# A conditioned transformer block: a quarter of fw1 reloaded, block 1's second LayerNorm a stage sooner, weight sums spread over three stages

## The chip, the core and the metric

The kernel runs on one core of one Trainium2 chip. The core has five engines that run at the same time, each with its own queue of instructions, which it takes strictly in order: TensorE (PE, matrix products; its weight loads are shown apart as PEld), VectorE (DVE), ScalarE (ACT), GpSimd (POOL) and SyncE (SP, which here only starts DMAs). An instruction whose inputs aren't there yet holds up everything behind it on its engine. The metric is the device time of one execution in microseconds (us), the median of three runs. In the profile, L599 means line 599 of the kernel's file.

## The reference

All data are float32. `x` is (2, 2048, 512), `t` (2, 512), and `h` = 1024. Cut to what is computed:

```python
emb = silu(t) @ ada_w + ada_b
shift_msa, scale_msa, gate_msa, shift_mlp, scale_mlp, gate_mlp = split(emb, 6)
norm = ln(x) * (1 + scale_msa) + shift_msa
x = x + gate_msa * (gelu(norm @ ssm_w1 + ssm_b1) @ ssm_w2 + ssm_b2)
norm2 = ln(x) * (1 + scale_mlp) + shift_mlp
x = x + gate_mlp * (gelu_tanh(norm2 @ ff_w1 + ff_b1) @ ff_w2 + ff_b2)
```

`ln` subtracts the mean of a row and divides by its standard deviation. The matrices are `ssm_w1`, `ssm_w2` (512 x 512; `w1`, `w2` in the kernel), `ff_w1` (512 x 1024; `fw1`) and `ff_w2` (1024 x 512; `fw2`).

## The kernel before

**Blocks and stages.** The 4096 rows of x are eight blocks of 512 rows (numbered 0 to 7; 0 to 3 belong to the first of the two conditions). Each block goes through four matrix stages, named after their tiles: hA (first product with w1, and gelu), oA (product with w2, added to x), hC (product with fw1, and gelu) and oC (product with fw2, added to x). TensorE runs them as hA_0, oA_0, hA_1, oA_1, hC_0, hA_2, oC_0, hC_1, oA_2, oC_1, hA_3 and so on, so that the vector work of one block lies beside the products of another.

**Products of halves.** A stage doesn't multiply whole matrices. Both operands are cut into quarters, called "11", "12", "21" and "22", and seven products P1 to P7 of quarters and of sums of quarters replace eight. `group` (L371) issues them in the order P1, P2, P6, P5, P7, P3, P4. P1, P6, P7 and P4 add into one bank of PSUM (y), P5 and P3 into another (v), P2 has its own (x). After each product `after` reads the bank: this is called a *take* here. Because the next product of the same bank adds into it, TensorE may start P6 only when P1's take has read, P7 only after P6's, P3 after P5's, and P4 after P7's. In hA and hC the takes are in `hidden` (L539), on VectorE, with gelus on ScalarE; in oA and oC they are in `residual` (L585), which adds into x on VectorE (L599).

**Sums.** Each operand needs four sums of quarters. `sums_of_first` (L307) writes "s1", then overwrites quarter "21" with "21" + "22", then writes "s0" and "s2"; `sums_of_second` (L316) writes "s1", overwrites "12", then writes "s0" and "s2". P6 reads "s0", P7 "s1", and P5 the overwritten quarter. For fw1 these four run once, on GpSimd, 128x1024 each (L310 to L313 with tiles `fw`, `fw_s`); likewise for fw2 (L320 to L323), after its eight k-slices were multiplied by the gate row (`fold5(0, 8)`, VectorE, L354; `fold5(8, 12)` are the four sums).

**Blocks 1 to 7 take another scheme for hC.** Instead of two groups of seven products, `Second.products` (L668) issues 26 smaller products (list `HK_P`), of 28 registers `fa` made from fw1 and 28 registers `fb[i]` made from the block's normalized rows. Registers 0 to 15 of `fa` are pieces of fw1 itself and 16 to 27 lie in the tile of its sums. Both are changed in place, by 37 sums of 128x256 for fw1 (`HK_A`, once, on VectorE, L634 and L636) and 20 sums for each block's rows (`HK_B`, on GpSimd for block 1). `HK_A` needs fw1 as it was loaded, not with its overwritten quarter, so fw1 is loaded a second time; and it can only begin when hC_0 no longer reads fw1.

**Second LayerNorm.** For block i, `Norm(i, 2)` (`n2[i]`) takes statistics of x (VectorE, four times L420 and L421), `scales` (eight tiny instructions on GpSimd, L429 to L447), four `normal` (ScalarE, L460), four `turn` (VectorE, 32x32 transposes into the tile `blocks`, L471), `move` (16 DMAs that finish the transposition, L480), and four `moved` (ScalarE, scale and shift, L503). The first LayerNorm of a block (`n1[i]`) goes the same way; for blocks 0 and 1 `normal(..., on_pe=True)` is followed by transposes on TensorE (`turned`).

**The order of the work around the products is written out by hand.** `hook(hooks, places, ops)` puts one operation after another behind the products named in `places` (the last place takes all that are left over). `group` calls them right after the product's take, and each lands in its engine's queue at that point. So a line such as `hook(hooks, ("P2", "P6", "P6", "P5"), st)` fixes where in VectorE's queue four statistics stand, and `take(n)` hands out the next n of the 37 sums of fw1.

Before the change the 37 sums stand as 4 in hA_2, 5 + 24 in oC_0 and 4 in hC_1.

## Time and profile before

| | us |
|---|---|
| median of three runs (615.16, 616.75, 614.74) | 615.16 |
| the profiled execution | 614.97 |
| its span, first to last instruction | 613.2 |

The profiled execution has some 1.8 us outside its span. The stages that the change touches, by the start of their first product: oA_0 at 30.19, hA_1 46.64, oA_1 59.92, hC_0 75.15 (its second half 87.75), hA_2 100.21, oC_0 112.30, hC_1 146.29, oA_2 170.34. Eight matmuls of 128x256 make one product of hA, oA or hC_0; undisturbed, products follow each other at 1.73 us (hA_2: 100.21, 101.94, 103.66, ...). In oC a product has sixteen matmuls and takes 3.45.

A timeline line reads: start, duration, engine, line, operation, tile written <- tiles read, shapes, count; in square brackets the idle time before it and who ended it. A line of a waits view reads: who <- on whom, us in total, how many times, the longest. A line of a windows view gives a stretch from:to, its length, the busy time of each engine in it with the count of instructions, TensorE's granted clock (1.00 is full), and DMA figures.

### The profile page before, as it was taken

What the parts mean: (1) busy time and instruction counts of PE and PEld (TensorE: products, weight loads), DVE (VectorE), ACT (ScalarE), POOL (GpSimd) and SP (SyncE); (2) the same over time, 40 slices, a digit from 0 to 9 for tenths busy, and PEclk for the clock granted to TensorE, in tenths of its full rate; (3) what the DMA queues carried; (4) which work ended last, traced back from release to release, by engine and by line L of the source; (5) the groups of instructions that cost most, each with busy time, mean ns of one, the idle gap of its engine ahead of it and who ended that gap; (6) DMA issues with size and microseconds to landing.
All of it is one profiled execution on the core that took longest, in us unless ns stands there. A gap on an engine that the chain in (4) does not pass through costs nothing.

```text
span 613.2 us, 8130 instructions
## 1 busy us (share of the span) xinstructions
PE 594.4 (97%) x2827; PEld 510.8 (83%) x2827; DVE 379.0 (62%) x641; ACT 216.6 (35%) x357; POOL 394.6 (64%) x445
## 2 busy tenths in 40 slices
PE   7999899968999999999999999999999999999997
PEld 4778788856888888888888888888888888888886
DVE  5968766999855456455666448744575336467642
ACT  3234335211641346222543236313462324212320
POOL 2866486996758399366996398895993695640110
PEclk9999999979999999999999999999999999999999
DMA  8980224221041201521022430413011310012001
GB/s 326 414 325 12 59 57 147 68 73 69 0 138 40 99 1 39 185 68 68 2 66 90 140 137 1 138 34 104 0 41 30 85 53 0 1 42 96 0 1 68
DMA packets 23371, 50.88 MB, mean 83 GB/s; under 512 B 4340, under 2 KB 4896, under 8 KB 22436
## 3 DMA queue, kind: packets, MB, share of 16 engines
q1 hardware_dynamic: 19648, 44.05, 21.3%
q10 hardware_dynamic: 3684, 6.33, 3.7%
q8 instruction: 22, 0.36, 0.2%
q14 instruction: 17, 0.14, 0.1%
HBM read 27.29 MB, written 8.39 MB: 58 GB/s over the span
## 4 chain that ended last, share of the span: by engine, by line
PE 84%; DVE 10%; issue 2%; DMA 2%; POOL 1%; ACT 1%; SPq 0%; POOLq 0%; DVEq 0%; ACTq 0%
PE py_oC L386 16%; PE px_hC L698 9%; PE pv_oC L386 8%; PE pv_hC L698 8%; PE py_hA L386 8%; PE py_hC L698 7%; PE py_oA L386 7%; PE pv_hA L386 4%; PE px_oC L386 4%; PE pv_oA L386 4%; DVE fw_s L636 2%; PE px_hA L386 2%; PE py_hC L386 2%; DVE fw L636 2%; PE px_oA L386 2%
## 5 line engine op out<-in xcount | busy, mean ns | idle before, releaser
L611 POOL TENSOR_TENSOR x<-x,gb 128x512 f32<-128x512 f32 x64 | 80.1, 1286 | 5.9 <-issue 2.1
L503 ACT ACTIVATE nT<-nT,mod,mod 128x512 f32<-128x512 f32 x54 | 39.6, 803 | 115.4 <-DMA nT<-blocks 115.4
L429 POOL TENSOR_SCALAR ve<-mv 128x4 f32<-128x4 f32 x16 | 3.7, 232 | 100.0 <-DVE mv L421 94.0
L386 PE MATMUL py_oC<-fw_s,hSC 128*128 128x256 f32 x256 | 59.6, 387 | 5.8 <-DVE x L599 5.8
L460 ACT ACTIVATE nT<-x,nmr,rstd 128x512 f32<-128x512 f32 x56 | 42.4, 803 | 55.7 <-POOL nmr L447 39.9
L386 PEld LDWEIGHTS py_oC<-fw_s,hSC 128*128 128x128 f32 x256 | 49.6, 195 | 13.5 <-DVE x L599 6.0
L310 POOL TENSOR_TENSOR hSC<-hClo 128x512 f32<-128x512 f32 x15 | 19.3, 1284 | 46.5 <-ACT hClo L693 37.8
L599 DVE TENSOR_TENSOR x<-py_oC,x 128x512 f32<-128x512 f32 (+1 forms) x36 | 22.5, 628 | 39.9 <-PE py_oC L386 39.9
L420 DVE BATCH_NORM_STATS2 st<-x 128x6 f32<-128x512 f32 x64 | 43.5, 679 | 5.0 <-DMA x<-in_x_dram 4.8
L698 PE MATMUL py_hC<-forms,fw 128*128 128x256 f32 x168 | 40.8, 379 | 0.0
L471 DVE STREAM_TRANSPOSE blocks<-nT 128x512 f32<-128x512 f32 x56 | 37.9, 694 | 3.9 <-ACT nT L460 3.4
L715 DVE TENSOR_TENSOR hClo<-hClo,py_hC 128x512 f32<-128x512 f32 x42 | 28.5, 681 | 17.0 <-ACT hClo L712 9.4
L636 POOL TENSOR_TENSOR forms<-forms 128x256 f32<-128x256 f32 x48 | 35.6, 741 | 2.8
L698 PEld LDWEIGHTS py_hC<-forms,fw 128*128 128x128 f32 x168 | 31.9, 190 | 4.3
L599 DVE TENSOR_TENSOR x<-py_oA,x 128x512 f32<-128x512 f32 x32 | 22.1, 690 | 20.5 <-PE py_oA L386 19.9
L715 DVE TENSOR_TENSOR hChi<-hChi,pv_hC 128x512 f32<-128x512 f32 x35 | 23.4, 684 | 17.1 <-PE pv_hC L698 17.1
L386 PE MATMUL py_oA<-w_s,hSA 128*128 128x256 f32 x128 | 30.4, 381 | 2.0 <-DVE hSA L312 2.0
L386 PE MATMUL py_oC<-fw_s,hChi 128*128 128x256 f32 x128 | 29.0, 380 | 1.7 <-DVE x L599 1.7
L386 PE MATMUL py_hA<-nS,w_s 128*128 128x256 f32 x128 | 30.3, 380 | 0.0
L386 PEld LDWEIGHTS py_oA<-w_s,hSA 128*128 128x128 f32 x128 | 24.2, 190 | 6.2 <-DVE hSA L312 2.4
L693 ACT ACTIVATE hClo<-hClo,colsT 128x256 f32<-128x256 f32 x56 | 25.3, 500 | 10.7 <-DVE hClo L715 10.5
L386 PE MATMUL pv_oC<-fw,hClo 128*128 128x256 f32 x128 | 28.9, 379 | 0.0
(228 smaller groups left out, 1429.0 us busy)
## 6 DMA issues: line engine op xcount, KB each, us to landing
nT<-blocks SPq DMA_DIRECT2D x160, 64.0 KB, 2.0
out_dram<-x SPq DMA_DIRECT2D x15, 512.0 KB, 3.0
x<-in_x_dram SPq DMA_DIRECT2D x7, 1024.0 KB, 7.1
ada<-in_L_cond_ada_w_dram SPq DMA_DIRECT2D x6, 1024.0 KB, 9.5
fw<-in_L_cond_ff_w_dram SPq DMA_DIRECT2D x3, 2048.0 KB, 9.0
nT<-blocks ACTq DMA_DIRECT2D x64, 64.0 KB, 2.1
w<-in_L_cond_ssm_w_dram SPq DMA_DIRECT2D x3, 1024.0 KB, 7.5
fw<-in_L_cond_ff_w_dram ACTq DMA_DIRECT2D x1, 2048.0 KB, 7.8
```

The source lines that it names most:

```text
L310: lambda: eng.tensor_tensor(s[1], q["11"], q["21"], ALU.subtract),
L386: nc.tensor.matmul(ps[b][j * apart][:, j, :], lhs(p, j, k), rhs(p, j, k), start=(fresh and j * (not apart) == 0 and k == 0), stop=(p in (" ...
L420: nc.vector.bn_stats(st, xs[self.i][:, c, :])
L460: nc.scalar.activation(t, x_c, AF.Identity, bias=self.nmr[:, c : c + 1], scale=self.rstd[:, c : c + 1])
L471: nc.vector.transpose(self.bl[:, :, :, c, :].rearrange("p m k q -> p k m q"), self.nT[:, c, :].rearrange("p (k m q) -> p k m q", k=KD, m=C),)
L503: nc.scalar.activation(dst, src, AF.Identity, bias=shift, scale=scale)
L599: nc.vector.tensor_tensor(d, ps[BANK[p]][:, js], d, ALU.add)
L611: lambda c=c: nc.gpsimd.tensor_tensor(xs[i][:, c, :], xs[i][:, c, :], gb, ALU.add)
L636: eng.tensor_tensor(reg[d], reg[a], reg[b], ALU.add if f == "+" else ALU.subtract)
L693: nc.scalar.activation(h, h, AF.Gelu_apprx_tanh, bias=fb1T[:, m : m + 1])
L698: nc.tensor.matmul(ps[b][:, j, :], fa[ra][:, j * P : (j + 1) * P], fb[rb].rearrange("p a (c q) -> p c a q", q=Q), start=(fresh and j == 0) ...
L715: nc.vector.tensor_tensor(dest(d), dest(d), ps[b], op)
```

## The change

It consists of these edits:

- **oA_0:** of n1[1]'s four `normal`, c = 0 and 2 stay on ScalarE behind P2; c = 1 and 3 go to VectorE (a `tensor_scalar`, L464), behind P6. fw1's third sum comes behind P4 of oA_0 (it stood in hA_1), its fourth behind P6 of oA_1.
- **oA_1:** on GpSimd, the first of n2[0]'s sums now stands ahead of n1[2]'s scales, the others behind; three of the eight folds of fw2 come here.
- **hC_0, first half:** block 1's statistics and scales, and the other five folds.
- **hC_0, second half:** block 1's four `normal` at once behind P1, its four `turn` and `move` (now all 16 DMAs on SP, before 8 on SP and 8 on ScalarE's queue); fw2's first sum ahead of n1[2]'s sums, the other three behind them; and `fw1_quarter`, which loads only quarter "21" of fw1 again (0.5 MB), where the whole 2 MB was loaded in hA_2.
- **hA_2:** block 1's `moved`; ten of the 37 sums on VectorE; the takes of P1, P6 and P5 go to ScalarE (`on_act`), two instructions each.
- **oC_0:** 18 of the sums; `HK_B` behind P1, the biases of block 2 behind P3. **hC_1:** the nine that are left.

```diff
+    def hidden(name, rhs, wops, bT, func, lo, hi, g, hooks, order=ORDER, on_act=False):
...
+        def take_first(dst, src, r):
+            if on_act:
+                for j in range(2):
+                    b = bT[:, r * half + m0 + j : r * half + m0 + j + 1]
+                    nc.scalar.activation(dst[:, j], src[:, j], AF.Identity, bias=b)
+            else:
+                nc.vector.tensor_tensor(dst, src, bias(r), ALU.add)
...
             if p == "P1":
-                nc.vector.tensor_tensor(s1, ps["y"], bias(0), ALU.add)
+                take_first(s1, ps["y"], 0)
...
             elif p == "P6":
-                nc.vector.tensor_tensor(u2, ps["y"], bias(0), ALU.add)
+                take_first(u2, ps["y"], 0)
             elif p == "P5":
-                nc.vector.tensor_tensor(s5, ps["v"], bias(1), ALU.add)
+                take_first(s5, ps["v"], 1)
...
-    hook(hooks, ("P2",), hA_sums[3:] + [lambda c=c: n1[1].normal(c, on_pe=True) for c in range(C)])
+    hook(hooks, ("P2",), hA_sums[3:] + [lambda c=c: n1[1].normal(c, on_pe=True) for c in (0, 2)])
+    hook(hooks, ("P6",), [lambda c=c: n1[1].normal(c, nc.vector) for c in (1, 3)])
     hook(hooks, ("P6",), [lambda: modulation(3, 1)])
...
     hook(hooks, ("P2",), fw1_sums[:1])
-    hook(hooks, ("P5",), fw1_sums[1:2])
+    hook(hooks, ("P5", "P4"), fw1_sums[1:3])
     residual("oA_0", 0, hA[0], w2_ops, KD // 2, hooks, order=FIRST)
...
-    hook(hooks, ("P2",), biases(1, gb[2]) + fw1_sums[2:])
+    hook(hooks, ("P2",), biases(1, gb[2]))
...
+    hook(hooks, ("P6",), fw1_sums[3:])
     hook(hooks, ("P2", "P6", "P6", "P5"), st)
-    hook(hooks, ("P5",), [n1[2].scales])
     hook(hooks, ("P6",), n2[0].moved())
-    hook(hooks, ("P5",), [ff_gate])
-    hook(hooks, ("P7",), n2[0].summed(nc.gpsimd) + [lambda c=c: n1[2].normal(c) for c in range(C)])
+    n2_sums = n2[0].summed(nc.gpsimd)
+    hook(hooks, ("P5",), [ff_gate] + n2_sums[:1] + [n1[2].scales])
+    hook(hooks, ("P7",), n2_sums[1:] + [lambda c=c: n1[2].normal(c) for c in range(C)])
+    hook(hooks, ("P7", "P3", "P4"), fold5(0, 3))
     turns = [lambda c=c: n1[2].turn(c) for c in range(C)]
     residual("oA_1", 1, hA[1], w2_ops, KD // 2, hooks)
...
-    hook(hooks, ("P3", "P4"), fold5(0, 2))
+    hook(hooks, ("P6", "P5", "P7", "P3"), n2[1].stats())
+    hook(hooks, ("P3",), [n2[1].scales])
+    hook(hooks, ("P6", "P5", "P7", "P3", "P4"), fold5(3, 8))
     hC.group(0, n2[0].ops, hooks)
+    def fw1_quarter():
+
+        half = slice(KH // 2 * P, KH * P)
+        nc.scalar.dma_start(
+            out=fw1_sb[:, : KD // 2, half], in_=fw1[: D // 2, half].rearrange("(k p) n -> p k n", p=P)
+        )
+
     hooks = {}
     hook(hooks, ("P1", "P1", "P2", "P6"), hC.summed(0, nc.gpsimd))
+    hook(hooks, ("P1",), [lambda c=c: n2[1].normal(c) for c in range(C)])
     hook(hooks, ("P2",), n1[2].moved())
-    hook(hooks, ("P6",), n1[2].summed(nc.gpsimd))
-    hook(hooks, ("P1", "P2", "P6", "P5"), n2[1].stats())
-    hook(hooks, ("P5",), [n2[1].scales])
-    hook(hooks, ("P1", "P2", "P6", "P5", "P7", "P3"), fold5(2, 8))
+    hook(hooks, ("P6",), fold5(8, 9) + n1[2].summed(nc.gpsimd) + fold5(9, 12))
+    hook(hooks, ("P5", "P7", "P3", "P4"), [lambda c=c: n2[1].turn(c) for c in range(C)])
+    hook(hooks, ("P5",), [fw1_quarter])
+    hook(hooks, ("P4",), [n2[1].move])
     hC.group(1, n2[0].ops, hooks)
...
-    hook(hooks, ("P1",), [lambda: load_w("fw1", fw1, fw1_sb, nc.scalar)])
-    hook(hooks, ("P1",), fold5(8, 12) + hC.summed(1, nc.gpsimd))
-    hook(hooks, ("P2", "P6", "P6", "P5"), [lambda c=c: n2[1].normal(c) for c in range(C)])
-    hook(hooks, ("P5", "P7", "P3", "P4"), [lambda c=c: n2[1].turn(c) for c in range(C)])
-    hook(hooks, ("P4",), [lambda: n2[1].move((nc.sync, nc.scalar))])
-    hook(hooks, ("P3", "P3", "P4", "P4"), take(4))
-    hA[2] = First(2, n1[2].ops, hooks)
+    hook(hooks, ("P1",), hC.summed(1, nc.gpsimd))
+    hook(hooks, ("P4",), n2[1].moved())
+    hook(hooks, ("P1", "P1", "P2", "P2", "P6", "P6", "P5", "P5", "P7", "P3"), take(10))
+    hA[2] = First(2, n1[2].ops, hooks, on_act=True)
     n1[3] = Norm(3, 1)
     hooks = {}
-    hook(hooks, ("P1",), [lambda: load_x(3)] + take(5))
-    hook(hooks, ("P1",), n2[1].moved() + biases(2, gb[2]))
+    hook(hooks, ("P1",), [lambda: load_x(3)])
     fb[1] = n2[1].registers()
-    hook(hooks, ("P2", "P6"), sums_of_registers(HK_B, fb[1], (nc.gpsimd,)))
-    hook(hooks, ("P2",) * 6 + ("P6",) * 5 + ("P5",) * 6 + ("P7",) * 4 + ("P3",) * 3, take(24))
+    hook(hooks, ("P1",), sums_of_registers(HK_B, fb[1], (nc.gpsimd,)))
+    hook(hooks, ("P3",), biases(2, gb[2]))
+    hook(hooks, ("P1",) * 4 + ("P2",) * 3 + ("P6",) * 4 + ("P5",) * 3 + ("P7",) * 2 + ("P3",) * 2, take(18))
     hook(hooks, ("P5", "P7", "P3", "P4"), n1[3].stats())
```

## The prediction, made before the changed kernel was run

> **What bounds the kernel now.** I read the page's busy shares first, then TensorE's waits, busy time by stage, and each engine's order of time around the waits.

> ```profile
> PE 594.4 (97%) x2827; PEld 510.8 (83%) x2827; DVE 379.0 (62%) x641; ACT 216.6 (35%) x357; POOL 394.6 (64%) x445
> ```

> TensorE is busy for 97% of the span and the change takes no matrix product away, so all it can win is TensorE's idle or slowed time. The waits say where that lies:

> ```profile
> PE py_oC L386 <- DVE x L599: 7.4, 3, 5.6
> ...
> PE py_oA L386 <- DVE hSA L312: 2.0, 1, 2.0
> ```

> By stage (length, then busy time of PE, PEld, DVE, ACT, POOL, then PE's clock): oC_0 and hC_1, and after them the same products in later blocks.

> ```profile
> 112.30:146.29 33.99, 26.54 (x113) 22.18 (x112) 33.54 (x41) 3.77 (x6) 31.30 (x30) 0.90 0.21 62
> 146.29:170.34 24.05, 23.03 (x106) 19.52 (x105) 19.86 (x37) 13.76 (x25) 16.66 (x19) 1.00 0.13 50
> 182.42:206.60 24.18, 24.18 (x114) 21.29 (x113) 12.03 (x24) 7.57 (x10) 12.49 (x16) 1.00 0.25 70
> 218.68:241.17 22.49, 22.49 (x106) 19.69 (x105) 15.34 (x24) 14.60 (x27) 21.05 (x22) 1.00 0.03 7
> ```

> oC_0 loses 33.99 - 24.18 = 9.8 us, hC_1 24.05 - 22.49 = 1.6. In oC_0 VectorE is busy 33.54 of 33.99: it sets the pace. Part of the 9.8 is clock (TensorE alone: length, busy, clock):

> ```profile
> 126.73:132.28 5.55, 0.00 (x1) 0.68 0.00 0
> 132.28:134.00 1.72, 1.72 (x4) 0.50 0.00 0
> 134.00:135.70 1.70, 1.70 (x5) 0.54 0.00 0
> 135.70:137.44 1.74, 1.74 (x9) 1.00 0.00 0
> ```

> After 5.55 us of idling the product P7 runs at half clock and takes 5.16 us (132.28 to 137.44) for 3.45: 1.7 more. The 2.0 us idle before 65.56 leaves the clock at 1.00.

> VectorE is slow because its sums wait for GpSimd:

> ```profile
> 110.76 2.42 POOL L322 TENSOR_TENSOR fw_s<-fw 128x1024 f32<-128x1024 f32 x1
> 113.25 2.47 POOL L323 TENSOR_TENSOR fw_s<-fw,fw_s 128x1024 f32<-128x1024 f32 x1
> ...
> 112.00 1.46 DVE L636 TENSOR_TENSOR fw<-fw 128x256 f32<-128x256 f32 x1
> 113.38 2.62 DVE L634 SCALAR_TENSOR_TENSOR fw<-fw 128x256 f32<-128x256 f32 x1
> 115.93 0.70 DVE L471 STREAM_TRANSPOSE blocks<-nT 128x512 f32<-128x512 f32 x1
> ```

> The first VectorE sum ends 0.28 us after GpSimd's first (113.18, 113.46), the second 0.28 after the next (115.72, 116.00). Alone such a sum takes 0.41. So a sum with both inputs in SBUF costs one GpSimd instruction: some 2.5 us beside 128x1024, 1.4 beside 128x512, 0.87 beside 128x256 (rows from 126 to 140). Transposes, statistics and anything that reads PSUM keep their 0.6 to 0.7.

> **The parts.** A product of 8 matmuls takes 1.727. T is the start of hC_0, 75.15 before.

> *Two of four normalizations to VectorE (oA_0).* The first four transposes take 40.03 to 41.87, 1.84, because ScalarE's normalizations run until 41.65; the second four take 0.44. So 1.4 is lost now. VectorE's form without GpSimd beside it, and the nearest one-stream row:

> ```profile
> L464 DVE TENSOR_SCALAR blocks<-x,rstd,nmr x2: 537/538/540, 10.7 to 11.2; 128x512 f32<-128x512 f32 x2
> ...
> L420 DVE BATCH_NORM_STATS2 st<-x 128x6 f32<-128x512 f32 x64 | 43.5, 679 | 5.0 <-DMA x<-in_x_dram 4.8
> ```

> If GpSimd doesn't hold them (as it doesn't hold L420), both end at 39.8, ScalarE's second at 40.23, and TensorE goes on at 40.6: 1.3 won. If it does, the first ends behind L323 (38.65 to 39.91) at 40.3, the second behind the next sum of 2.4 at 42.8, TensorE goes on at 43.05: 1.2 lost. No row shows it. 512 elements in 538 ns is faster than any one-stream row (about 680), which speaks for a second path, so I put it with the held sums: **+1.2**, from -1.3. P7's take and the modulation queued behind have 1 us to spare.

> [...] No row here shows this instruction beside GpSimd.

> *fw1's sums earlier.* At 59.9 VectorE's hSA sums wait behind two fw1 sums (1.70 and 2.72 for 0.67), and TensorE waits at 65.56: 65.56 - 61.65 - 1.73 = 2.2. Now one of these is done a stage before; only the first hSA sum is held, the third ends at 63.4, when TensorE wants it: **-2.1**. The third sum of n2_0 is taken apart by the scales of n1_2: ScalarE's modulates end at 69.9, then on GpSimd a sum of 1.3, the scales of 3.05 (71.39 to 74.44 now) and two sums of 1.35: ready at 77.05. TensorE wants it two products into hC_0, at 75.15 - 2.1 + 3.45 = 76.5, and waits 0.55; now it is 79.01 against 78.60, 0.4: **+0.1**. The three folds of oA_1 (0.585 from one to the next) go into VectorE's pauses there, 1.03 before each take; without these pauses they would cost 1.8.

> *Block 1's statistics and five folds in hC_0's first half.* VectorE's queue from the end of P1 (T+1.95): take 0.60, gate 0.60, two transposes of 0.61, P2's take, two transposes, so that P6's take begins at T+6.2. From there each product brings a take 0.60, a statistic 0.81 and a fold 0.585, which is 2.0 (as from 89.67 to 91.67 now) for TensorE's 1.73: P5's take begins at T+8.2, P7's at T+10.2 and ends at T+10.9. P4 adds into the same bank and wants it at six products and the 0.55, T+10.9: nothing lost, with nothing to spare. P3's take begins at T+12.2, the last statistic ends at T+13.7. The second half has only transposes left beside the takes, and its wait at 98.38 (after 96.39 + 1.73) goes: **-0.3**. On ScalarE four normalizations now stand in front of the second half's first gelu and n1_2's modulates: they wait for the scales (T+16.8), then 4 x 0.71, a gelu 0.6 and 4 modulates of 0.71 end at T+23.2, covered by GpSimd, which comes to n1_2 only at T+24.6; scales later by more than 1.4 would show.

> *GpSimd's chain.* Last statistic T+13.7, scales 3.05, four hC sums of 1.35, one fw2 sum of 2.45 (T+24.6), three n1_2 sums to T+28.7. hA_2's P6 comes after 16 products, 16 x 1.727 + 0.55 = T+28.1: **+0.6**.

> *hA_2.* Ten fw1 sums on VectorE, eight of them in its queue ahead of P7's take. GpSimd goes on with an n1_2 sum (T+30.1), three fw2 sums of 2.5 (T+37.6), hC sums of 1.4 (two by T+40.4). Sums 3 to 8 each take one of these: sum 8 ends at T+40.7, the take at T+41.4. P4 adds into the bank that the take reads and wants it after 20 products and the waits above, 20 x 1.727 + 0.55 + 0.6 = T+35.7: 5.7, and 0.1 to pass the word on: **+5.8**. Bounds: 0 if the sums (0.34 each alone) slip in, 9.2 if each loses to two. An idle time this long cost 1.7 of clock above: **+1.7** (bounds 0 and 1.7). The three takes given to ScalarE (0.84 a pair, L571's row) fit with their table load of 1.28 between products; without the cover of a product each would cost its 0.84.

> *Quarter load, move.* The quarter (0.5 MB) leaves at about T+22; 512 KB land in 5.2 us, the first reader is sum 5 at T+33. SP alone now issues 16 moves: n1_2's took 13.1 from the last transpose to the first modulate (81.29, 94.38), so T+38.2, under P4's gelus at T+43. Nothing; without the stall the gelus would end at T+38.3 and the cover be gone, at a cost to HK_B's start only. x_3's load and block 0's stores stand behind these moves on SP, but x_3 waits for hA_2's last product anyway, and lands (7.1) long before oC_0's P5, where its first statistic is.

> *oC_0.* VectorE: seven takes 4.2, 18 sums beside HK_B at 0.87, 15.7, four statistics 3.2: 23.1 of 24.18. The worst place is P1, 0.60 + 4 x 0.87 = 4.1 for 3.45, and P2's three sums after it; the takes fall behind by about 1 us, and each bank is wanted only one product of 3.45 later: nothing lost, **-9.8**. HK_B starts when the modulates end (T+48.7 with the clock's 1.7) and takes 20 x 0.87: T+66, before hC_1 starts at T+69. The biases of x_2, which stood in front of HK_B, follow it (4 x 1.35, T+71.5); oA_2 reads x_2 over 20 us later, so they cost nothing but the place of n1_3's scales and hA_2's sums behind them.

> *hC_1.* Nine sums, not four, in the first nine products. The first four fall beside the small scales (0.3 to 0.9), the rest beside 128x512 sums (1.4). Then banks are late at products 8, 12 and 14: 2.0 to 3.7 lost by how the two queues meet; I take 2.3 for 1.6: **+0.7**.

> Sum: 1.2 - 2.1 + 0.1 - 0.3 + 0.6 + 5.8 + 1.7 - 9.8 + 0.7 = -2.1. Span 613.2 becomes 611.1; the run with its 1.8 around, 612.9; the median stands 0.19 above that run: **613.0**.

> **Rivals.** *GpSimd doesn't hold the normalizations:* -2.5 more, 610.5. For it: one SBUF stream. Against: 538 ns. *hA_2's sums hide:* no stall there and no clock, -7.5, 605.5. It needs VectorE to slip in between; the rows above speak against. *Slower: GpSimd wins the port twice for each VectorE sum.* In hA_2 GpSimd's work ends at T+43.2, so the take ends at most 3.4 later; in oC_0 ten sums instead of twenty pass beside HK_B's 17 us and P6's take is late, some 5: +8.4, 621. It decides once these add over 4 us. Against: one for one from 112 to 126.

> **Numbers.** This kernel's measurement tells apart about 0.3%, 1.85 us. Forecast 0.48 (own range 611.3 to 615.0, which straddles that bound: 0.29 faster, 0.19 same), unheld 0.25, hidden 0.06, twice 0.09; the remaining 0.12 is the forecast's sum with hC_1 at 3.7 and half a us more in hA_2, 615, same. Faster 0.60, same 0.31, slower 0.09. The range 609.3 to 615.6 leaves out the hidden and the slow case.

> **What would show it.** The L599 wait of 5.55 gone, oC_0 at 24.2 and clock 1.00; a new TensorE wait of 5 to 6 us on VectorE's L564 take in hA_2 with half clock behind it; normalizations on VectorE of 1.5 and 2.5 us, not 0.54; no hSA wait. I am wrong if L564 isn't late, or if oC_0 still waits.

## The result, and the profile after

| us | before | changed |
|---|---|---|
| median of 14 runs each, on one chip | 615.15 | 615.11 |
| lowest and highest | 614.19 to 617.26 | 613.02 to 618.06 |
| the profiled execution | 614.97 | 615.28 |
| its span | 613.2 | 613.5 |

The ratio is 0.9996 with a 95% interval of 0.9978 to 1.0014: no change that can be told. The forecast of 613.0 is 2.1 low; the time lies inside its range of 609.3 to 615.6, 0.5 below the upper end.

The large parts did what they should, and they cancel. By stage, each from the start of its first product to the start of the next stage's, in the two profiled executions:

| stage | before | changed | difference | forecast |
|---|---|---|---|---|
| oA_0 (to hA_1's start, 46.64 and 49.37) | | | +2.73 | +1.2 |
| oA_1 | 15.23 | 13.20 | -2.03 | -2.1 |
| hC_0 | 25.06 | 24.81 | -0.25 | -0.2 |
| hA_2 | 12.09 | 19.96 | +7.87 | +8.1 |
| oC_0 | 33.99 | 24.94 | -9.05 | -9.8 |
| hC_1 | 24.05 | 25.09 | +1.04 | +0.7 |
| sum | | | +0.31 | -2.1 |

The row of hA_1 is left out, 13.28 in both. What is gained or lost stands by the end of hC_1: oA_2 begins at 170.65 (before: 170.34), and the span is 0.3 longer. TensorE's waits in the changed kernel, who <- on whom, us, times, longest:

```profile
PE py_hA L386 <- DVE hA L573: 5.5, 1, 5.5
PE pt L489 <- DVE blocks L464: 2.0, 1, 2.0
```

The waits on L599 (5.55 in oC_0) and on hSA (2.0) are gone. In their place stand one of 5.5 on a take of hA_2, and one of 2.0 on the normalizations that moved to VectorE. First that smaller one (timeline: start, us, engine, what; in brackets the idle time before):

```profile
38.73 3.97 DVE L464 TENSOR_SCALAR blocks<-x,rstd,nmr 128x512 f32<-128x512 f32 x2 [0.76 <-POOL nmr L447]
...
38.66 1.27 POOL L323 TENSOR_TENSOR w_s<-w,w_s 128x512 f32<-128x512 f32 x1
39.89 2.53 POOL L310 TENSOR_TENSOR fw_s<-fw 128x1024 f32<-128x1024 f32 x1
...
40.02 0.69 PE L489 MATMUL pt<-ident,blocks 128*128 128x128 f32 x3
42.76 0.33 PE L489 MATMUL pt<-ident,blocks 128*128 128x128 f32 x1 [2.04 <-DVE blocks L464]
42.92 2.90 PE L386 MATMUL pv_oA<-w,hSA 128*128 128x256 f32 x8
```

GpSimd's sum began 0.07 ahead of the two normalizations; they last 3.97 together (1.49 and 2.56, overlapping a little) and end 0.28 after GpSimd's second sum (42.42, 42.70). Alone such an instruction takes 0.54. TensorE starts P3 (the last line) at 42.92, 1.05 later than before (41.87), near the 1.2 of the forecast. But its span in that line is 2.90, where the kernel before shows 1.89:

```profile
41.71 0.33 PE L489 MATMUL pt<-ident,blocks 128*128 128x128 f32 x1 [0.38 <-ACT blocks L460]
41.87 1.89 PE L386 MATMUL pv_oA<-w,hSA 128*128 128x256 f32 x8
```

Windows of the changed kernel's stretch (from:to, length, busy time of PE, PEld, DVE, ACT, POOL, then TensorE's clock) say why:

```profile
38.90:42.76 3.86, 1.81 (x10) 1.12 (x10) 3.86 (x3) 1.35 (x2) 3.78 (x3) 1.00 1.01 403
42.76:47.30 4.54, 4.54 (x16) 3.77 (x17) 2.33 (x5) 1.36 (x2) 4.46 (x2) 0.62 0.08 34
```

After the idle time the clock is down, 0.62 on average; from P3 to hA_1 it takes 6.45 instead of 4.77: **1.68 that the forecast didn't have.** In hA_2:

```profile
105.87 2.57 DVE L645 TENSOR_TENSOR fw_s<-fw 128x256 f32<-128x256 f32 x1
108.48 2.49 DVE L645 TENSOR_TENSOR fw_s<-fw_s,fw 128x256 f32<-128x256 f32 x1
110.89 2.63 DVE L645 TENSOR_TENSOR fw_s<-fw 128x256 f32<-128x256 f32 x1
113.56 2.77 DVE L645 TENSOR_TENSOR fw_s<-fw_s,fw 128x256 f32<-128x256 f32 x2
116.25 0.68 DVE L573 TENSOR_TENSOR hA<-py_hA,hA 128x512 f32<-128x512 f32 x1
...
105.62 2.54 POOL L321 TENSOR_TENSOR fw<-fw 128x1024 f32<-128x1024 f32 x1
108.24 2.45 POOL L322 TENSOR_TENSOR fw_s<-fw 128x1024 f32<-128x1024 f32 x1
110.77 2.47 POOL L323 TENSOR_TENSOR fw_s<-fw,fw_s 128x1024 f32<-128x1024 f32 x1
113.21 1.44 POOL L310 TENSOR_TENSOR hSC<-hClo 128x512 f32<-128x512 f32 x1
114.72 1.33 POOL L311 TENSOR_TENSOR hClo<-hClo,hChi 128x512 f32<-128x512 f32 x1
...
109.65 1.89 PE L386 MATMUL pv_hA<-nT,w_s 128*128 128x256 f32 x8
117.08 3.75 PE L386 MATMUL py_hA<-nS,w 128*128 128x256 f32 x8 [5.54 <-DVE hA L573]
120.62 4.38 PE L386 MATMUL py_oC<-fw,hClo 128*128 128x256 f32 x16
```

Sum by sum, VectorE ends 0.28 after GpSimd (108.16 and 108.44; 110.69 and 110.97; 113.24 and 113.52): these sums (L645) stand ahead of P7's take in VectorE's queue, and P4 needs that take (L573; it was L564 before the change). P4 starts at 117.08, T + 41.23 with T = 75.85; the forecast had the take end at T + 41.4 and P4 start 0.1 later. P4 then lasts 3.54 (to 120.62) for 1.73, and oC_0's P1 4.22 (to 124.84) for 3.45: 1.81 + 0.77 = 2.58 of half clock, where the forecast had 1.7. And the stage that was to win, and the one behind it:

```profile
120.62:145.56 24.94, 24.94 (x113) 21.86 (x112) 19.52 (x30) 3.65 (x6) 20.42 (x23) 0.97 0.05 21
145.56:170.65 25.09, 23.25 (x105) 19.51 (x104) 22.37 (x36) 13.77 (x25) 19.18 (x22) 1.00 0.09 29
```

oC_0 has no waiting left; all of its 24.94 over 24.18 is that 0.77. VectorE, busy 33.54 of 33.99 before, is busy 19.52.

### The profile page after: what moved, and what is told of

It reads as the page before. It is cut to its first block, busy times and chain, and to the rows that moved or that the text cites. A ratio compares the mean times of both kernels' runs of the same rounds, so it can differ in the third digit from the quotient of the medians.

```text
span 613.5 us, 8128 instructions
## 1 busy us (share of the span) xinstructions
PE 596.5 (97%) x2827; PEld 512.7 (84%) x2827; DVE 382.6 (62%) x640; ACT 217.3 (35%) x361; POOL 394.7 (64%) x445
## 4 chain that ended last, share of the span: by engine, by line
PE 87%; DVE 6%; DMA 2%; POOL 1%; issue 1%; ACT 1%; ACTq 1%; SPq 0%; DVEq 0%
PE py_oC L386 18%; PE pv_oC L386 9%; PE px_hC L707 9%; PE py_hA L386 8%; PE pv_hC L707 8%; PE py_hC L707 7%; PE py_oA L386 7%; PE px_oC L386 5%; PE pv_oA L386 4%; PE pv_hA L386 4%; PE px_hA L386 2%; PE py_hC L386 2%; PE px_oA L386 2%; DMA ada<-in_L_cond_ada_w_dram 2%; DVE fw_s L645 2%
## 5 line engine op out<-in xcount | busy, mean ns | idle before, releaser
L386 PE MATMUL py_oC<-fw_s,hSC 128*128 128x256 f32 x256 | 57.9, 379 | 0.0
L386 PEld LDWEIGHTS py_oC<-fw_s,hSC 128*128 128x128 f32 x256 | 48.6, 190 | 6.6
L420 DVE BATCH_NORM_STATS2 st<-x 128x6 f32<-128x512 f32 x64 | 43.4, 678 | 5.2 <-DMA x<-in_x_dram 4.9
L471 DVE STREAM_TRANSPOSE blocks<-nT 128x512 f32<-128x512 f32 x56 | 37.8, 694 | 3.8 <-ACT nT L460 3.5
L645 POOL TENSOR_TENSOR forms<-forms 128x256 f32<-128x256 f32 x48 | 35.5, 740 | 2.8
L386 PE MATMUL py_hA<-nS,w_s 128*128 128x256 f32 x128 | 30.4, 381 | 0.1
L386 PE MATMUL py_oA<-w_s,hSA 128*128 128x256 f32 x128 | 30.4, 381 | 0.0
L702 ACT ACTIVATE hClo<-hClo,colsT 128x256 f32<-128x256 f32 x56 | 25.4, 500 | 13.8 <-DVE hClo L724 13.7
L386 PE MATMUL py_oC<-fw,hClo 128*128 128x256 f32 x128 | 29.7, 386 | 0.0
L386 PE MATMUL pv_oC<-fw,hSC 128*128 128x256 f32 x128 | 28.9, 379 | 0.0
L386 PE MATMUL py_oC<-fw_s,hChi 128*128 128x256 f32 x128 | 28.9, 379 | 0.0
```

Source lines behind the costliest of these rows:

```text
L386: nc.tensor.matmul(ps[b][j * apart][:, j, :], lhs(p, j, k), rhs(p, j, k), start=(fresh and j * (not apart) == 0 and k == 0), stop=(p in (" ...
L420: nc.vector.bn_stats(st, xs[self.i][:, c, :])
L471: nc.vector.transpose(self.bl[:, :, :, c, :].rearrange("p m k q -> p k m q"), self.nT[:, c, :].rearrange("p (k m q) -> p k m q", k=KD, m=C),)
L645: eng.tensor_tensor(reg[d], reg[a], reg[b], ALU.add if f == "+" else ALU.subtract)
L702: nc.scalar.activation(h, h, AF.Gelu_apprx_tanh, bias=fb1T[:, m : m + 1])
```

## The experiments

Four theories were to be told apart or confirmed: that GpSimd's instruction holds VectorE's, in oA_0 and in hA_2 ("port theory" is the author's name for it; the runs can show the hold, they show no port); that the clock behind the idle time is a cost of its own; and that hA_2's place in VectorE's queue, not the number of sums, makes the long wait. Each kernel is an edit of the changed one. The kernel before ran beside them on the same chip, median 615.17 beside the first three and the long filler and 614.99 beside the others.

**All four normalizations back on ScalarE** (`e1_norms_scalar`).

```diff
-    hook(hooks, ("P2",), hA_sums[3:] + [lambda c=c: n1[1].normal(c, on_pe=True) for c in (0, 2)])
-    hook(hooks, ("P6",), [lambda c=c: n1[1].normal(c, nc.vector) for c in (1, 3)])
+    hook(hooks, ("P2",), hA_sums[3:] + [lambda c=c: n1[1].normal(c, on_pe=True) for c in range(C)])
```

> All four normalizations of block 1 back on ScalarE, all else as in the change. Port and clock (my theory): the changed kernel lost 2.7 us before hA_1 (49.37 against 46.64) because the second VectorE normalization waits behind two GpSimd sums and the clock then halves; undone, hA_1 starts at 46.6 to 46.7, the clock stays at 1.00 there, and the run is 2.7 shorter, about 612.4. Rival (later stages have slack that took the 2.7 up): hA_1 earlier, but the run the same, 615.

Measured: 612.18 (611.98 to 612.40), ratio 0.995 [0.9936, 0.9965]. hA_1 begins at 46.66, as before the change (46.64), and the wait of 5.6 in hA_2 is unchanged. So this one edit costs the whole 2.7 of oA_0, and the rest of the change is worth 3.0 without it.

**Six of hA_2's ten sums behind P7's take** (`e2_take_first`).

```diff
-    hook(hooks, ("P1", "P1", "P2", "P2", "P6", "P6", "P5", "P5", "P7", "P3"), take(10))
+    hook(hooks, ("P1", "P1", "P2", "P2", "P7", "P7", "P7", "P7", "P3", "P3"), take(10))
```

> In hA_2 six of the ten sums stand behind P7's take (four) and P3's take (two) instead of four ahead of it; as many sums in every stage as in the change. Queue theory: the wait of 5.5 us for L573 falls below 0.5, no half clock follows, oC_0 starts 8 us earlier, hC_1 loses up to 1 us more; about 607.5. Rival (VectorE simply has too much to do beside GpSimd, wherever the sums stand): the wait comes back in oC_0 or hC_1, within 1 us of 615.

Measured: 609.34, ratio 0.9897 [0.9865, 0.9929], 1.8 above the expected 607.5, from runs of 606.31, 608.14, 610.53 and 610.61. The wait on L573 is gone with the same ten sums: the place in the queue made it. The sums themselves are no faster; beside GpSimd's 128x1024 ones they still take 2.6 (from 104.06 and from 109.11), but no longer ahead of a take that TensorE is about to need. (hC_1, reached sooner, is 26.24 long for 25.09.) The runs lie 4.3 apart, and their mean clocks go with them: 1.000, 0.997, 0.994, 0.992. The profiled one is the fastest, and there the clock stayed up behind the very same idle time in oA_0:

```profile
42.63 0.33 PE L489 MATMUL pt<-ident,blocks 128*128 128x128 f32 x1 [2.04 <-DVE blocks L464]
42.79 1.89 PE L386 MATMUL pv_oA<-w,hSA 128*128 128x256 f32 x8
```

From P3 (42.79) to hA_1 (47.56) it is 4.77 here, 6.45 in the changed kernel's profiled execution. So the clock halved behind these 2.0 us without a product in one profiled execution and not in the other; the last section shows what tells them apart.

**GpSimd's sums held back until the normalizations are done** (`e3_gpsimd_held`). A tiny GpSimd instruction that reads the last normalized row stands ahead of its sums.

```diff
-    hook(hooks, ("P1",), hA_sums[2:3] + st[2:] + [n1[1].scales] + fold2(7, 8))
+    hook(hooks, ("P1",), hA_sums[2:3] + st[2:] + [n1[1].scales])
...
+    def hold():
+        t = small.tile([P, C], F32, tag="held", name="held", bufs=1)
+        nc.gpsimd.tensor_scalar(t, n1[1].xn[:, 3, :C], EPS, None, ALU.add)
...
+    hook(hooks, ("P6",), [hold] + fold2(7, 8) + fw1_sums[:1])
...
-    hook(hooks, ("P2",), fw1_sums[:1])
-    hook(hooks, ("P5", "P4"), fw1_sums[1:3])
+    hook(hooks, ("P7", "P4"), fw1_sums[1:3])
```

> As the change, but on GpSimd a tiny instruction that reads the last VectorE normalization of block 1 stands ahead of w2's last sum and fw1's first one, so that GpSimd is idle while VectorE normalizes. Port theory: the two normalizations take 0.54 each instead of 3.97 together, end near 39.8, P3 of oA_0 starts near 40.6 at clock 1.00, hA_1 near 45.3; about 611. Rival (their length is their own, or they wait for something else): still some 4 us together, 615.

Measured: 613.69, ratio 0.9974 [0.9962, 0.9986].

```profile
38.52 1.00 DVE L464 TENSOR_SCALAR blocks<-x,rstd,nmr 128x512 f32<-128x512 f32 x2 [0.72 <-POOL nmr L447]
...
39.60 0.23 POOL L850 TENSOR_SCALAR held<-blocks 128x4 f32<-128x4 f32 x1 [1.12 <-DVE blocks L464]
39.89 1.27 POOL L323 TENSOR_TENSOR w_s<-w,w_s 128x512 f32<-128x512 f32 x1
```

The same two instructions take 1.00 when GpSimd stands still, 3.97 when it doesn't: the hold is shown for them. hA_1 begins at 45.13, 4.2 earlier than in the changed kernel. But GpSimd's sums now run later and hold VectorE later:

```profile
PE pv_hA L386 <- DVE nT L321: 0.9, 1, 0.9
...
PE py_oA L386 <- DVE hSA L312: 0.3, 1, 0.3
```

So 1.8 us was given back within two stages (hA_1 14.75 long for 13.28, oA_1 13.56 for 13.20), 1.2 of it in these two waits, and the expected 611 missed.

**Three of fw2's four sums left out** (`e5_no_fw2_sums`): GpSimd then runs 128x512 sums where it ran 128x1024 ones.

```diff
-    hook(hooks, ("P6",), fold5(8, 9) + n1[2].summed(nc.gpsimd) + fold5(9, 12))
+    hook(hooks, ("P6",), fold5(8, 9) + n1[2].summed(nc.gpsimd))
...
+    hook(hooks, ("P6",), fw1_sums[3:] + [lambda: nc.gpsimd.memset(fw2_s, 0.0)])
```

> As the change, but three of fw2's four sums on GpSimd are left out (128x1024 each, between the last sum of n1_2 and the first sum of hC_0's second half), and the tile of fw2's sums is zeroed beforehand, so oC's products read other numbers. Port theory: sums 4 to 8 then wait for GpSimd's 128x512 sums (1.4) instead of 2.5 each, P7's take in hA_2 ends some 4.7 us sooner and TensorE waits about 1 us at P4 instead of 5.5, with no half clock behind it. Rival (the sums are late by themselves, or wait for the reloaded quarter of fw1): the wait at P4 stays 5 to 6 us.

Measured, in one run: 608.73.

```profile
105.93 1.49 DVE L645 TENSOR_TENSOR fw_s<-fw 128x256 f32<-128x256 f32 x1
107.45 1.38 DVE L645 TENSOR_TENSOR fw_s<-fw_s,fw 128x256 f32<-128x256 f32 x1
108.75 1.48 DVE L645 TENSOR_TENSOR fw_s<-fw 128x256 f32<-128x256 f32 x1
...
112.73 1.97 PE L386 MATMUL py_hA<-nS,w 128*128 128x256 f32 x8 [1.13 <-DVE hA L573]
```

The same VectorE sums fall from 2.5 to 1.4 with GpSimd's instruction, the wait from 5.5 to 1.1, and P4 behind 1.1 of waiting runs at full clock. The length of GpSimd's instruction is the price of a VectorE sum here. (The profiled execution keeps the wait of 2.0 in oA_0, with P3 at half clock behind it: 3.41, from 42.88 to 46.29, for 1.73.)

**The idle time filled with products that nobody reads** (`e4_filler`, then `e9_filler_fitted`). TensorE multiplies the identity by itself into a spare bank while it waits, in oA_0 ahead of the last transpose and in hA_2 ahead of P4. The waits stay; only the clock can change.

```diff
+    def filler(n):
+        t = ps_t.tile([P, C, P], F32, tag="t", name=f"filler_{n}")
+        for _ in range(n):
+            nc.tensor.matmul(t, ident, ident.unsqueeze(1).to_broadcast([P, C, P]), start=True, stop=True)
...
+                if (self.name, k, c) == ("1_1", 0, 3):
+                    filler(4)
...
+    hook(hooks, ("P3",), [lambda: filler(12)])
```

> As the change, with unused 128x512 products that keep TensorE busy in its two gaps: 4 ahead of the last transpose of the first four in oA_0 (1.7 us in a gap of 2.0) and 12 ahead of P4 in hA_2 (5.2 in 5.5). Clock theory: both waits stay, but P3 of oA_0 takes 1.73 instead of 2.7, P4 of hA_2 1.73 instead of 3.5 and oC_0's P1 3.45 instead of 4.2; 4 us less, about 611. Rival (these products are slow for another reason, operands or banks): they stay slow, 615 or a little more.

Measured: 616.96, ratio 1.0037 [1.0022, 1.0052], slower instead of 611. The filler was too long: 12 such products last 10.3, 0.86 each, and four last 3.4; they overfill the gaps of 5.5 and 2.0. The clock did stay up (P4 took 1.73, from 120.99 to 122.72). The fitted version has `filler(2)` and `filler(6)`:

> As the filler run, with half the products (2 in oA_0, 6 in hA_2), since a 128x512 product showed 0.86 us of TensorE, twice what the first filler was sized for: 1.7 us in a gap of 2.0, 5.2 in one of 5.5. Clock theory: both waits still end where they do in the change, P4 of hA_2 then takes 1.73 and oC_0's P1 3.45 (2.6 less), P3 of oA_0 1.73 (up to 1.7 less): 611 to 613, with little spread between runs, since all stay at clock 1.00. Rival: 615, the same spread as the change.

Measured: 611.46, ratio 0.9947 [0.9927, 0.9966].

```profile
111.83 5.31 PE L410 MATMUL filler<-ident 128*128 128x512 f32 x12
117.57 1.97 PE L386 MATMUL py_hA<-nS,w 128*128 128x256 f32 x8 [0.43 <-DVE hA L580]
119.37 3.62 PE L386 MATMUL py_oC<-fw,hClo 128*128 128x256 f32 x16
```

(The count x12 is of six products, each recorded as two.) P4 still begins behind VectorE's take, but it now takes 1.80 and the next product 3.45, where the changed kernel needs 3.54 and 4.22; in oA_0, P3 takes 1.73 again. Three of its four runs lie within 611.23 to 611.61 at a mean clock of 0.999 or 1.000; the fourth, the profiled one, took 613.68 and was 2.1 late already ahead of the edits (oA_0's P7 at 40.33, in the changed kernel 38.19): its clock stood at 0.50 from 11.87 to 15.28, and hA_0's first product began at 16.08 for 14.57. Against the changed kernel's profiled 615.28 the three are 3.7 to 4.1 us shorter, by no other means than keeping TensorE busy: nearly all of the 1.68 and 2.58, together 4.26, that were put down to the clock.

**Both repairs** (`e7_both`: the normalizations on ScalarE and the takes first, the diffs of the first two experiments together).

> The normalizations of block 1 all on ScalarE, and in hA_2 six of ten sums behind the takes of P7 and P3: both edits of the first two experiments. If the two losses are separate, hA_1 starts at 46.66, hA_2 loses no time, no long idle time is left up to hC_1 and the clock is 1.00 throughout: 605.5, with little spread. Rival (they are the same slack seen twice, the later one limits): 608 to 609.

Measured: **605.55** (605.28 to 605.79), ratio **0.9842 [0.9829, 0.9856]**, as expected, and the best of all. The mean clock is 0.999 or 1.000 in all five runs, and they agree within 0.5 us. What remains is in hC_1, 26.23 long for 22.49:

```profile
PE px_hC L707 <- ACT hClo L721: 1.3, 1, 1.3
PE py_hC L707 <- DVE hClo L724: 0.8, 1, 0.8
```

**One sum fewer in hA_2 and in hC_1, two more in oC_0** (`e8_both_respread`).

```diff
-    hook(hooks, ("P1", "P1", "P2", "P2", "P7", "P7", "P7", "P7", "P3", "P3"), take(10))
+    hook(hooks, ("P1", "P1", "P2", "P2", "P7", "P7", "P7", "P3", "P3"), take(9))
...
-    hook(hooks, ("P1",) * 4 + ("P2",) * 3 + ("P6",) * 4 + ("P5",) * 3 + ("P7",) * 2 + ("P3",) * 2, take(18))
+    hook(hooks, ("P1",) * 3 + ("P2",) * 4 + ("P6",) * 4 + ("P5",) * 3 + ("P7",) * 3 + ("P3",) * 3, take(20))
```

> As the run with both edits, but 9, 20 and 8 sums in hA_2, oC_0 and hC_1 instead of 10, 18 and 9, the nine with three behind P7 and two behind P3. oC_0 has some 1 us of VectorE time free and its banks 3.4 us of slack, hC_1 has none, so one sum fewer there should save up to 0.9: hC_1 from 26.2 to 25.5, 604.8. Rival: hC_1's waits come from its own reads, no change.

Measured: 607.18, ratio 0.987 [0.985, 0.989]; a miss. The two sums added at oC_0's end fall beside GpSimd's biases and cost 1.4 to 1.5 each, as these lines from around hC_1's start (134.31) show:

```profile
133.76 1.38 DVE L645 TENSOR_TENSOR fw_s<-fw_s,fw 128x256 f32<-128x256 f32 x1
135.06 1.49 DVE L645 TENSOR_TENSOR fw_s<-fw 128x256 f32<-128x256 f32 x1
...
137.28 0.66 DVE L608 TENSOR_TENSOR x<-py_oC,x 128x512 f32<-128x512 f32 x1
```

oC_0's last take comes at 137.28, 2.5 later than in the kernel with both repairs (134.75), so VectorE enters hC_1 further behind, the wait on L721 grows from 1.3 to 1.9, and hC_1 is 26.94 long for 26.23. That is 0.7 in the profiled execution, the fastest (606.00, mean clock 0.999); the other three, 606.56 to 608.61, have mean clocks of 0.994 to 0.997, so most of the 1.6 between the medians is likely the clock's; they weren't profiled. No other spread was tried; whether hC_1's 3.7 can be won by one is open.

## Why the prediction was right and where its sum was off

Its main mechanisms held, term by term, and the clock made its sum 2.1 too low. What it thought most likely, a kernel that is faster (0.60), didn't come: the measured time is the same, to which it gave 0.31. That the time lies in the range owes something to luck: the narrower range for the sum alone, 611.3 to 615.0, misses 615.11 by 0.1, and the case of 615 that the forecast did allow was to come from hC_1 and hA_2, not from the clock. (The sum itself, 615.16 - 2.1, gives 613.06, put down as 613.0.)

- *hA_2's stall*, forecast +5.8: +5.70, and P4's start within 0.3 of the forecast's (T + 41.23 for T + 41.5). The queue walk that let each sum cost one GpSimd instruction was right; the leave-out run shows it.
- *hSA in oA_1*, -2.1: -2.03. *oC_0*, -9.8: -9.8 once the 0.77 of clock that runs into it is taken off. hC_0's two small terms, -0.2: -0.25; P6 of hA_2, +0.6: +0.26.
- *hC_1*, +0.7: +1.04. Its loss is 2.6, inside the bounds of 2.0 to 3.7 but above the 2.3 taken. With both repairs it is 3.7, the upper bound.
- *Normalizations on VectorE*, +1.2: +2.73. The hold was right: 1.05, with VectorE's end at 42.70 where 42.8 was forecast. The rival in which GpSimd doesn't hold them falls with the held-back run: 1.00 without GpSimd, 3.97 with it. What failed is a step that came before the sum: "The 2.0 us idle before 65.56 leaves the clock at 1.00" was taken as a rule and applied to an idle time of the same length, so nothing was charged. It cost 1.68. The reader of one profiled execution couldn't see that the same gap can go either way; but 0 should have been one end of a range and 1.7 the other, as it was for hA_2.
- *The clock behind hA_2's stall*, +1.7: +2.58. It had been sized by one earlier instance, and its upper bound of 1.7 was the mis-sized one. The half clock lasts 6.83 both times, but before the change 3.54 of it passed while TensorE still waited (128.74 to 132.28), here only 1.75 (115.33 to 117.08), so that more products ran slowly.

Of the miss of 2.4 in the profiled span (+0.31 for -2.1), the clock is 1.68 + 0.88 = 2.56, hC_1 0.34; the hold in oA_0, P6 of hA_2 and hA_2's stall came out 0.6 under the forecast together. The changed kernel's 14 runs say the same from outside: the five at a mean clock of 0.994 took 613.02 to 614.07, those at 0.989 took 617.43 to 618.06. The forecast of 613.0 is the time of an execution in which the clock fell least. That these five are the ones without the fall in oA_0 is likely by their size, and because the kernel with all normalizations on ScalarE, profiled at the same 0.994, shows the one fall in hA_2 only; but they weren't profiled.

The slower rival, in which GpSimd wins twice for each sum, is out: in hA_2 VectorE got one sum in after each of its instructions. That in which hA_2's sums slip in between is out too. With the takes first TensorE doesn't wait either, but for another reason: a sum there still takes up to 2.6, but no take that TensorE is about to need stands behind it.

## What to carry to other kernels

In this kernel a VectorE sum of two operands in SBUF took about as long as the GpSimd instruction beside it (2.5 to 2.6 beside 128x1024, 1.4 to 1.5 beside 128x512, 0.41 alone), and two scalar operations on a whole row took 1.49 and 2.56 for 0.54. Price such work at one GpSimd instruction, and put the takes that TensorE waits for ahead of it: the same ten sums cost 5.5 us of waiting in one order of their stage and none in the other. Price a TensorE stall at its length plus the half clock behind it (here 2.58 behind 5.5 us), and for a stall of about 2 us keep both cases (here 1.68 in one execution, nothing in another). Work moved from a slow engine to a faster one is only won if it isn't held there, as the 0.54 that became 1.49 and 2.56 was.

## What the runs showed of the hardware

| kernel, place | TensorE busy in the slice | the clock then |
|---|---|---|
| before, oC_0 | 1.40 (125.32 to 128.74) | 0.50 until 135.56 |
| changed, oA_0 | 1.36 (40.25 to 43.66) | 0.50 until 47.07 |
| changed, hA_2 | 0.00 (111.92 to 115.33) | 0.50 until 122.16 |
| before, the 2.0 us ahead of 65.56 | 3.07 (60.47 to 63.88), 1.73 (63.88 to 67.29) | 1.00 |
| takes first, the 2.0 us in oA_0 | 1.92 (38.66 to 42.07), 2.86 (42.07 to 45.49) | 1.00 |

  So the 2.0 us halved the clock where all of it lay in one slice (40.71 to 42.76 in the changed kernel), and didn't where a slice's border cut it (63.88 in 63.60 to 65.56; 42.07 in 40.59 to 42.63). Where the borders fell differed from execution to execution: the last row and the second are the same gap.
- The half clock lasted whole slices. In oA_0 it lasted one, with 3.41 of work in it, and 1.68 is lost; in hA_2 it lasted two, the first of them (115.33 to 118.75) with only 1.67 of work and the second with 3.41, and 2.58 is lost. Before the change it lasted two, with 0.00 and 3.28. So in these two executions a slice at half clock with 1.67 or less was followed by another, and one with 3.28 or more by full clock. Nor was the slice ahead of the fall always idle: it held 1.36 and 1.40 us of work in two of the three places.
- Products that nobody reads kept the clock up in the two waits: the run gained 3.7 to 4.1 us where they fit the gaps, and was 1.8 us slower than the kernel before where they didn't, at 0.86 for each 128x512 float32 product.
- The spread between runs of one kernel went with this clock: 5.0 us in the changed kernel with its two idle times, mean clocks 0.989 to 0.994; 0.5 us with both repairs, 0.999 or 1.000. The respread kernel has neither idle time and still spreads by 2.6, at 0.994 to 0.999. Its waits in hC_1 leave a stretch of 3.41 us with only 1.13 of work (140.60 to 144.01; with both repairs the least there is 1.57), so a slice that falls there would, by the table, be followed by half clock (an estimate: 1.13 is below its 1.36 and 1.40). That this made its slower runs is not shown; they weren't profiled.
